# Layer 1's expert feed-forward, worked in smaller first groups, two experts at a time, and dealt out by amount of work

## The chip, the cores and the metric

The kernel runs on one core of one Trainium2 chip. The metric is device microseconds (us) for one execution. Three runs of the kernel before took 4180.68, 4183.84 and 4184.01 us; the median is 4183.84 us.

## The reference, cut to what matters

A graph of 6250 nodes (256 features each) and 100000 edges, sorted by destination node, goes through two layers. Each layer is a graph step and then a mixture of experts, and each adds to the node features `x`:

```python
x = x + L0_gnn(layernorm(x), ...)                # weighted graph convolution and a small MLP
x = x + L0_ffn(layernorm(x), ...)                # 8 experts, top 2
x = x + L1_gnn(edge_index, layernorm(x), ...)    # the table and sums below
x = x + L1_ffn(layernorm(x), ...)                # the feed-forward below

# L1_gnn: a table of 8 relations, gathered by edge and summed by destination
hx = einsum('ni,rio->rno', x, weight);  msg = hx[edge_type, src]
agg = segment_sum(msg, dst);  out = agg * 0.5**0.5 + h_bias + (x @ loop_weight) * 0.5**0.5

# L1_ffn: 6 experts of three 256x256 products each, all computed for every node
rh = relu(f @ router_w1 + b);  logits = softmax(rh @ router_w2 + b);  top 2, softmax of the two
h1 = relu(f @ w1[e] + b1[e]);  h2 = relu(h1 @ w2[e] + b2[e]);  y = h2 @ w3[e] + b3[e]
out = sum over the two chosen experts of weight * y
```

Here `f` is `layernorm(x)` after the graph step. A node's feed-forward can begin only when all of its edges have been summed.

## The kernel before, in words

Nodes lie in 49 tiles of 128. The kernel's stages follow each other: layer 0's messages and sums, its experts, the relation table `hx` (line 1425, matmuls from 2459.9 to 2907.8 us), and then the last stage, which the change touches and which runs from about 2913 us to the end.

In that last stage two things are interleaved. The function `aggregate` (line 906) makes 830 turns. A turn gathers 128 rows of the table with one indirect DMA, issued by POOL (line 920, tile `g1`, 10 buffers); multiplies them on PE by a 0/1 selection matrix `m1` with three bf16 matmuls (line 928, `pa1`); and adds the result to the accumulator of one node tile on DVE (line 932). The matrix `m1` is made on DVE once in 8 turns (line 912). Edges are sorted by node, so tile after tile is completed, one every 17 turns or so.

The other thing is layer 1's feed-forward over groups of node tiles. `FFN_GROUPS` lists the groups; before, they have 2 tiles, then eleven times 4, then 2 and 1. A group passes two generators. `prepare` (line 1466) adds the graph sums to the features, normalizes, transposes on PE (`pt_x3`), runs the router (`pqa`, `pl3`), the softmax and the top 2 (`route`, `shares`, on DVE and ACT; the result is the table of weights `C`), transposes `C` (`pc1`, line 1520) and adds the weighted bias (`pcb1`, line 1527). `experts1` (line 1533) then takes the six experts in turn: two dense products, in two halves each (`dense_steps`, line 470: `ph_e1` and `ph_e2` on PE, a relu on ACT, line 482, into `v1` and `v2`), and a third product for every tile (`mix`, line 1003: `py1` on PE, line 1007, and a multiply-add on DVE, line 1008). A `yield` ends a piece of it.

The PSUM pool `mm`, with 4 buffers, serves `pa1`, `ph`, `py1`, `pqa` and `pcb1` alike; whoever needs a buffer waits until ACT or DVE has read it out.

The function `layer1` (line 1555) decides the order. After each turn of `aggregate` it may start the next group's preparation, if that group's last tile is complete for certain (`TURNS * sum(waiting[0]) + SLACK <= turn`, that is turn 17 x tiles + 8) and fewer than `LIVE - 1` = 2 groups stand in the queue; it advances the running preparation by one step; and it deals out pieces of expert work from an account `due`, which grows each turn by `left / (T - turn + 40)`. Before, every piece counts as one, whatever its size: with 4 tiles all pieces hold two units of work, a unit being a pair of matmuls with 256 columns; with 2 tiles the dense pieces hold one unit. When the 830 turns are over, a loop empties the queue. The framework that builds the program may shift instructions within an engine's queue[...].

Of the kernel before, what the change touches and what calls it, by code (L numbers as in the profile page):

```python
# [8 lines left out]
F32 = mybir.dt.float32  # L9
# [5 lines left out]
AF = mybir.ActivationFunctionType  # L15
# [7 lines left out]
NT = 49  # L23
# [5 lines left out]
T = C_ + NT - 1  # L29
# [19 lines left out]
TABLE_GROUPS = [(0, 1)] + [(g, 4) for g in range(1, NT, 4)]  # L49

LIVE = 3
SIZES = [2] + [4] * 11 + [2, 1]
FFN_GROUPS = [(sum(SIZES[:i]), n) for i, n in enumerate(SIZES)]


@with_exitstack
def gnn_ffn_kernel(ctx: ExitStack, tc: tile.TileContext, a, out):
    nc = tc.nc
# [36 lines left out]
    last = N - (NT - 1) * 128  # L95
# [32 lines left out]
    col0, n = {}, 0  # L128
# [19 lines left out]
    def col(name, i=0):  # L148
        j = col0[name] + i
        return cols[:, j : j + 1]  # L150
# [66 lines left out]
    with tc.If(unsorted > 0):  # L217
        with tc.tile_pool(name="reorder", bufs=1) as rp:
# [22 lines left out]
            for c in range(EC):  # L241
                ins = nc.gpsimd.indirect_dma_start(
                    out=records,
# [69 lines left out]
    for q0 in range(0, QN, 4):  # L313
        n = min(4, QN - q0)
# [37 lines left out]
    turn = gap.tile([128, Q * 128], F32, name="turn")  # L352
# [35 lines left out]
    for q in range(Q):  # L388
        nc.gpsimd.indirect_dma_start(
            out=M[:, q].rearrange("p e r -> p (e r)"),  # L390
# [79 lines left out]
    def dense_steps(name, w, xT, ncols, func, bias, dest):  # L470

        for f in range(2):
            ps = psum_mm(f"ph_{name}_{f}")
            for k in range(2):
                nc.tensor.matmul(  # L475
                    ps[:, :ncols],
                    w[:, k, f * 128 : (f + 1) * 128],
                    xT[:, k, :ncols],
                    start=(k == 0),
                    stop=(k == 1),  # L480
                )
            nc.scalar.activation(dest[:, f, :ncols], ps[:, :ncols], func, bias=bias[f])  # L482
            yield
# [519 lines left out]
    def mix(s, t, i, e, C, hT, j, w):  # L1003

        ps = psum_mm(f"py{s}_{t}_{e}")
        for k in range(2):
            nc.tensor.matmul(ps[:, :D], hT[:, k, j : j + 128], w[:, k, :], start=(k == 0), stop=(k == 1))  # L1007
        nc.vector.scalar_tensor_tensor(  # L1008
            X[:, t, :], ps[:, :D], C[:, i, e : e + 1], X[:, t, :], op0=OP.mult, op1=OP.add
        )  # L1010
# [393 lines left out]
    tiles = []  # L1404
# [61 lines left out]
    def prepare(g, n, va, tag):  # L1466


        tiles = range(g, g + n)
        m = n * 128  # L1470
        mv = va.tile([128, n, 2], F32, name=f"mv3{tag}_{g}", tag="mv3", bufs=2)
        for i, t in enumerate(tiles):
            nc.vector.scalar_tensor_tensor(
                X[:, t, :], acc[:, t * D : (t + 1) * D], math.sqrt(0.5), X[:, t, :], op0=OP.mult, op1=OP.add
            )
            st = work.tile([128, 6], F32, name=f"st3{tag}_{t}", tag="st", bufs=3)
            nc.vector.bn_stats(st, X[:, t, :])
            nc.vector.bn_aggr(mv[:, i, :], st)
            yield
        rstd = va.tile([128, n], F32, name=f"rstd3{tag}_{g}", tag="rstd3", bufs=2)  # L1480
        inverse_root(f"ln3{tag}_{g}", va, mv[:, :, 1], rstd, n)
        yield
        xT = va.tile([128, 2, 512], F32, name=f"xT3{tag}_{g}", tag="xT3", bufs=LIVE)
        normed = []
        for i in range(n + 1):
            if i < n:
                t = g + i
                xn = work.tile([128, D], F32, name=f"xn3{tag}_{t}", tag="xn", bufs=3)
                nc.vector.tensor_scalar(
                    xn, X[:, t, :], mv[:, i, 0:1], rstd[:, i : i + 1], op0=OP.subtract, op1=OP.mult  # L1490
                )
                normed.append(xn)
            if i:
                transpose_to(f"x3{tag}_{g + i - 1}", xT[:, :, (i - 1) * 128 : i * 128], normed[i - 1])
            yield
        yield
        ps = psum_mm(f"pq{tag}{g}")
        for k in range(2):
            nc.tensor.matmul(ps[:, :m], qw1[:, k, :], xT[:, k, :m], start=(k == 0), stop=(k == 1))
        q = va.tile([128, 512], F32, name=f"q{tag}{g}", tag="q", bufs=1)  # L1500
        nc.scalar.activation(q[:, :m], ps[:, :m], AF.Relu, bias=col("L1_ffn_router_b1"))
        yield
        yield
        pl = psum_sm(f"pl3{tag}_{g}")
        for i in range(n):
            nc.tensor.matmul(
                pl[:, i * 8 : i * 8 + 6], q[:, i * 128 : (i + 1) * 128], qw2, start=True, stop=True
            )
        yield
        L = va.tile([128, n, 6], F32, name=f"L3{tag}_{g}", tag="L3", bufs=2)  # L1510
        nc.vector.tensor_add(
            L, pl[:, : n * 8].rearrange("p (n e) -> p n e", e=8)[:, :, :6], qb2.to_broadcast([128, n, 6])
        )
        C = shares(f"1{tag}{g}", va, n, 6, *(yield from route(f"1{tag}{g}", va, L, n, 6, True)))
        yield
        yield

        pc = psum_sm(f"pc1{tag}_{g}")
        for i in range(n):
            nc.tensor.transpose(pc[:6, i * 128 : (i + 1) * 128], C[:, i, :], ident)  # L1520
        cT = va.tile([8, 512], F32, name=f"cT1{tag}_{g}", tag="cT", bufs=1)
        nc.scalar.copy(cT[:6, :m], pc[:6, :m])
        yield
        yield
        for i, t in enumerate(tiles):
            ps = psum_mm(f"pcb1{tag}_{t}")
            nc.tensor.matmul(ps[:, :D], cT[:6, i * 128 : (i + 1) * 128], vb3, start=True, stop=True)
            nc.vector.tensor_add(X[:, t, :], X[:, t, :], ps[:, :D])
            if i % 2:
                yield  # L1530
        return xT, C

    def experts1(g, n, va, tag, xT, C):

        tiles = range(g, g + n)
        m = n * 128
        for e in range(6):
            h1 = va.tile([128, 2, 512], F32, name=f"v1{tag}_{g}_{e}", tag="actT", bufs=1)
            h2 = va.tile([128, 2, 512], F32, name=f"v2{tag}_{g}_{e}", tag="hid", bufs=1)
            b1 = [col("L1_ffn_expert_b1", 2 * e + f) for f in range(2)]  # L1540
            b2 = [col("L1_ffn_expert_b2", 2 * e + f) for f in range(2)]
            yield from dense_steps(f"e1{tag}_{g}_{e}", vw1[:, e], xT, m, AF.Relu, b1, h1)
            yield from dense_steps(f"e2{tag}_{g}_{e}", vw2[:, e], h1, m, AF.Relu, b2, h2)
            for i, t in enumerate(tiles):
                mix(f"1{tag}", t, i, e, C, h2, i * 128, vw3[:, e])
                if e == 5:
                    r = last if t == NT - 1 else 128
                    nc.sync.dma_start(out[t * 128 : t * 128 + r, :], X[:r, t, :])
                if i % 2 or i == n - 1:
                    yield  # L1550

    def pieces(n):
        return 6 * (4 + (n + 1) // 2)

    def layer1(tag, early):


        with tc.tile_pool(name=f"gather{tag}", bufs=1) as gp, tc.tile_pool(name=f"act{tag}", bufs=1) as va:
            waiting = list(FFN_GROUPS)
            prep, queue = None, []  # L1560
            left = sum(pieces(n) for _, n in waiting[:-2])

            def prepare_some():

                nonlocal prep
                if prep is None:
                    return False
                g, n, steps = prep
                try:
                    next(steps)  # L1570
                except StopIteration as end:
                    queue.append(experts1(g, n, va, tag, *end.value))
                    prep = None
                return True

            def experts_some():
                while queue:
                    if next(queue[0], queue) is not queue:
                        return True
                    queue.pop(0)  # L1580
                return False

            due = 0.0
            for turn in aggregate(gp, acc, hx, tag):
                if not early:
                    continue
                if prep is None and waiting and len(queue) < LIVE - 1 and TURNS * sum(waiting[0]) + SLACK <= turn:
                    g, n = waiting.pop(0)
                    prep = (g, n, prepare(g, n, va, tag))
                prepare_some()  # L1590
                due = min(due + left / (T - turn + 40), 1.5)
                while due >= 1 and experts_some():
                    due, left = due - 1, left - 1
            while prep or waiting or queue:
                if prep is None and waiting and len(queue) < LIVE:
                    g, n = waiting.pop(0)
                    prep = (g, n, prepare(g, n, va, tag))
                prepare_some()
                experts_some()
# [62 lines left out]
```

## Time and profile before

| what | value |
|---|---|
| median of three runs | 4183.84 us |
| the profiled execution's own time | 4184.38 us |
| its span, first to last instruction | 4182.6 us |
| PE / DVE / ACT / POOL busy over the span | 83% / 50% / 31% / 54% |
| last stage: first and last gather issued | 2920.3 and 4060.0 us |
| last stage: first and last matmul of the gathered sums | 2925.5 and 4073.8 us |
| first expert matmul (`ph_e1`) | 3008.0 us |
| last expert matmul (`py1`) | 4176.4 us |

Times inside the span are counted from its first instruction. The profile gives, per stretch of time, the busy time of each engine and the clock that TensorE was granted (1.00 is full speed). It also gives every instruction's start, so that the three `pa1` matmuls of a turn tell when PE reached that turn, and the gather's start tells when POOL did; the difference, in turns, is called the lead of the gathers below. It can't exceed the 10 buffers.

### The profile page before, as it was taken

Reading aid. Unit: us, or ns where it says so; the run is one execution under the profiler, and the core shown is the slowest. Engines: PE = TensorE matmul, PEld = TensorE weight load, DVE = VectorE, ACT = ScalarE, POOL = GpSimd, SP = SyncE. Lnnn points to the kernel's source line nnn. Section 1 sums busy time; section 2 is a strip of 40 time slices with the busy share of each in tenths; the row PEclk is TensorE's granted clock in tenths of the full one; section 3 lists DMA queues with packets and bytes.
Section 4 is the critical chain, followed back from the end, with each engine's and each line's share of the span. In section 5 each row is a group of like instructions: output and inputs, shape, how many; then the busy total and the mean of one; then the engine's idle time right before and its main releaser. Section 6 shows DMA issues by size and latency. Waiting matters only on the chain.

```text
span 4182.6 us, 53223 instructions
## 1 busy us (share of the span) xinstructions
PE 3478.2 (83%) x14645; PEld 2313.5 (55%) x14645; DVE 2083.1 (50%) x5720; ACT 1310.2 (31%) x2934; POOL 2261.2 (54%) x2440
## 2 busy tenths in 40 slices
PE   2887777777777568888969967998679999999999
PEld 1565656655656345555547733444356666666656
DVE  6686211111111146777853367664456666666652
ACT  3312333333333212333324434665012222222213
POOL 1001777777777524555550057333767777777750
PEclk8998999999999788999989988999689999999999
DMA  5514433333333434555643335445645555555540
GB/s 178 170 38 148 131 128 127 128 128 127 127 127 128 159 102 158 191 201 188 214 165 108 109 122 199 196 196 201 187 140 152 151 153 153 147 154 153 146 115 9
DMA packets 233067, 612.09 MB, mean 146 GB/s; under 512 B 41908, under 2 KB 126103, under 8 KB 212783
## 3 DMA queue, kind: packets, MB, share of 16 engines
q0 software_dynamic: 100624, 294.88, 22.7%
q1 hardware_dynamic: 112636, 290.21, 20.8%
q10 hardware_dynamic: 19488, 23.31, 1.6%
q8 instruction: 132, 2.16, 0.2%
q14 instruction: 187, 1.53, 0.1%
HBM read 371.49 MB, written 236.79 MB: 145 GB/s over the span
## 4 chain that ended last, share of the span: by engine, by line
PE 41%; DVE 12%; DMA 5%; issue 5%; POOL 2%; ACT 2%; DVEq 1%; ACTq 0%; SPq 0%; POOLq 0%
PE ph_e1a L475 6%; PE py1a L1007 6%; PE pa1a L928 6%; PE ph_e2a L475 5%; PE pa0e L901 4%; PE phx L1425 4%; DMA g0e<-msgs 3%; DVE acc L903 3%; PE pf L1344 2%; PE pf L1360 2%; DVE rest L1435 1%; DVE acc L932 1%; PE pt_fh L463 1%; DVE hx L1419 1%; PE pg2e L1094 1%
## 5 line engine op out<-in xcount | busy, mean ns | idle before, releaser
L860 POOL DMA_INDIRECT msgs<-msgn,at x782 | 787.4, 1007 | 550.3 <-DMA M<-edge_table,natq_i 313.6
L920 POOL DMA_INDIRECT g1a<-hx,idxT x830 | 828.6, 998 | 319.1 <-PE pa1a L928 142.5
L842 PE MATMUL pxn<-acc,sTn 128*128 x3128 | 792.2, 413 | 242.1 <-DVE sTn L823 215.3
L842 PEld LDWEIGHTS pxn<-acc,sTn 128*128 128x128 f32 x3128 | 613.9, 206 | 420.3 <-DVE sTn L823 282.2
L901 PE MATMUL pa0e<-g0e,m0e 128*128 128x256 f32 x1660 | 503.3, 436 | 157.5 <-DVE acc L903 71.8
L857 ACT ACTIVATE msgn<-pxn,ewT 128x256 f32<-128x256 f32 x782 | 370.1, 473 | 638.5 <-PE pxn L842 468.0
L932 DVE TENSOR_TENSOR acc<-acc,pa1a 128x256 f32 x830 | 346.7, 418 | 341.8 <-PE pa1a L928 309.8
L901 PEld LDWEIGHTS pa0e<-g0e,m0e 128*128 128x128 f32 x1660 | 293.0, 207 | 330.6 <-issue 128.5
L898 POOL TENSOR_SCALAR m0e<-minus,keye 128x128 f32<-128x128 f32 x414 | 259.5, 641 | 320.0 <-PE pa0e L901 275.7
L833 DVE COPY msgn<-srcT 128x32 f32<-128x32 f32 x98 | 17.5, 181 | 831.1 <-DMA msgs<-msgn,at 722.1
L928 PE MATMUL pa1a<-g1a,m1a 128*128 128x256 bf16 x2490 | 375.6, 283 | 51.6 <-DMA g1a<-hx,idxT 35.0
L928 PEld LDWEIGHTS <-m1a 128*128 128x128 bf16 x2490 | 244.0, 100 | 275.2 <-issue 192.3
L903 DVE TENSOR_TENSOR acc<-acc,pa0e 128x256 f32 x830 | 347.2, 418 | 92.7 <-PE pa0e L901 42.9
L1425 PE MATMUL phx<-wr,xT 128*128 128x512 f32 x784 | 368.5, 613 | 29.1 <-DVE rest L1435 21.6
L1007 PE MATMUL py1a<-w_L_ffn_expert_w,v2a 128*128 128x256 f32 x1176 | 286.6, 384 | 6.0 <-DVE acc L932 3.0
L475 PE MATMUL ph_e1a<-xT3a,w_L_ffn_expert_w 128*128 128x512 f32 (+2 forms) x672 | 287.9, 555 | 0.0
L475 PE MATMUL ph_e2a<-v1a,w_L_ffn_expert_w 128*128 128x512 f32 (+2 forms) x672 | 280.1, 542 | 2.1 <-DVE acc L932 1.3
L482 ACT ACTIVATE v1a<-ph_e1a,cols 128x512 f32<-128x512 f32 (+2 forms) x168 | 106.5, 634 | 538.8 <-PE ph_e1a L475 525.7
L1425 PEld LDWEIGHTS phx<-wr,xT 128*128 128x128 f32 x784 | 148.2, 197 | 188.5 <-issue 161.2
L1385 POOL DMA_INDIRECT y<-ys,ats x98 | 97.5, 995 | 277.5 <-issue 262.2
L1007 PEld LDWEIGHTS py1a<-w_L_ffn_expert_w,v2a 128*128 128x128 f32 x1176 | 208.8, 190 | 44.2 <-ACT v2a L482 10.3
L1008 DVE SCALAR_TENSOR_TENSOR X<-py1a,C1a,X 128x256 f32<-128x256 f32 x294 | 138.9, 480 | 112.3 <-PE py1a L1007 111.4
(646 smaller groups left out, 4373.2 us busy)
## 6 DMA issues: line engine op xcount, KB each, us to landing
g0e<-msgs SPq DMA_DIRECT2D x104, 1040.0 KB
hx<-hx SPq DMA_DIRECT2D x49, 1536.0 KB
rowsn<-lane_rows SPq DMA_DIRECT2D x98, 256.0 KB
fx<-xs SPq DMA_DIRECT2D x105, 128.0 KB
ys<-fy ACTq DMA_DIRECT2D x105, 128.0 KB
g1a<-hx,idxT POOLq DMA_INDIRECT x830, 3.1
msgs<-msgn,at POOLq DMA_INDIRECT x782, 2.4
msgs<-none ACTq DMA_DIRECT2D x10, 650.0 KB
```

What stands on the lines that cost most here:

```text
L475: nc.tensor.matmul(ps[:, :ncols], w[:, k, f * 128 : (f + 1) * 128], xT[:, k, :ncols], start=(k == 0), stop=(k == 1),)
L842: nc.tensor.matmul(come, sT[:, k, j, :], acc[:, bass.ds(blocks[j] * D + k * D, D)], start=(k == 0), stop=(k == 1),)
L857: nc.scalar.activation(msg[:, j, :D], come, AF.Copy, scale=ewT[:, t0 + j : t0 + j + 1])
L860: ins = nc.gpsimd.indirect_dma_start(out=msgs, out_offset=bass.IndirectOffsetOnAxis(ap=at[:, t0 + j : t0 + j + 1], axis=0), in_=msg[:, j, ...
L898: nc.gpsimd.tensor_scalar(m[:, j], minus, key[:, j : j + 1], None, op0=OP.is_equal)
L901: nc.tensor.matmul(ps[:, :D], m[:, j, :], g[:, j, :D], start=True, stop=True)
L903: nc.vector.tensor_add(here, here, ps[:, :D])
L920: nc.gpsimd.indirect_dma_start(out=g, out_offset=None, in_=table, in_offset=bass.IndirectOffsetOnAxis(ap=idxT[:, t0 + j : t0 + j + 1], axi ...
L928: nc.tensor.matmul(ps[:, :D], m[:, j, :], g[:, k * D : (k + 1) * D], start=(k == 0), stop=(k == 2))
L932: nc.vector.tensor_add(here, here, ps[:, :D])
L1007: nc.tensor.matmul(ps[:, :D], hT[:, k, j : j + 128], w[:, k, :], start=(k == 0), stop=(k == 1))
L1425: nc.tensor.matmul(ps, xT[:, k, :], wr[:, k, r : r + 2, :].rearrange("p r o -> p (r o)"), start=(k == 0), stop=(k == 1),)
```

## The change

Four edits. The groups begin smaller: 1, 2, 2, 3 tiles, then nine times 4, then 2, 2, 1. In groups of one or two tiles `experts1` takes two experts together: both first products, then both second products, then both mixes, side by side in the same `v1` and `v2` buffers; larger groups go through the same sequence as before. A piece now hands out its size in units of work, the account of `layer1` counts these units, may run up to 3.0, and deals while it is above zero. And `prepare` has one more `yield` between the weights `C` and their transpose, so that a preparation lasts one turn longer.

```diff
-SIZES = [2] + [4] * 11 + [2, 1]
+SIZES = [1, 2, 2, 3] + [4] * 9 + [2, 2, 1]
 FFN_GROUPS = [(sum(SIZES[:i]), n) for i, n in enumerate(SIZES)]
...
         C = shares(f"1{tag}{g}", va, n, 6, *(yield from route(f"1{tag}{g}", va, L, n, 6, True)))
         yield
         yield
+        yield
...
     def experts1(g, n, va, tag, xT, C):
         tiles = range(g, g + n)
         m = n * 128
-        for e in range(6):
-            h1 = va.tile([128, 2, 512], F32, name=f"v1{tag}_{g}_{e}", tag="actT", bufs=1)
-            h2 = va.tile([128, 2, 512], F32, name=f"v2{tag}_{g}_{e}", tag="hid", bufs=1)
...
-            yield from dense_steps(f"e1{tag}_{g}_{e}", vw1[:, e], xT, m, AF.Relu, b1, h1)
-            yield from dense_steps(f"e2{tag}_{g}_{e}", vw2[:, e], h1, m, AF.Relu, b2, h2)
-            for i, t in enumerate(tiles):
-                mix(f"1{tag}", t, i, e, C, h2, i * 128, vw3[:, e])
...
-    def pieces(n):
-        return 6 * (4 + (n + 1) // 2)
+        some = 2 if n <= 2 else 1
+        for e0 in range(0, 6, some):
+            h1 = va.tile([128, 2, 512], F32, name=f"v1{tag}_{g}_{e0}", tag="actT", bufs=1)
+            h2 = va.tile([128, 2, 512], F32, name=f"v2{tag}_{g}_{e0}", tag="hid", bufs=1)
+            parts = [(e0 + c, slice(256 * c, 256 * c + m)) for c in range(some)]
+            for e, cs in parts:
+                b1 = [col("L1_ffn_expert_b1", 2 * e + f) for f in range(2)]
+                for _ in dense_steps(f"e1{tag}_{g}_{e}", vw1[:, e], xT, m, AF.Relu, b1, h1[:, :, cs]):
+                    yield n / 2
+            for e, cs in parts:
+                b2 = [col("L1_ffn_expert_b2", 2 * e + f) for f in range(2)]
+                for _ in dense_steps(f"e2{tag}_{g}_{e}", vw2[:, e], h1[:, :, cs], m, AF.Relu, b2, h2[:, :, cs]):
+                    yield n / 2
+            for e, cs in parts:
+                for i, t in enumerate(tiles):
+                    mix(f"1{tag}", t, i, e, C, h2, cs.start + i * 128, vw3[:, e])
...
+                    if i % 2 or i == n - 1:
+                        yield 1 + i % 2
...
-            left = sum(pieces(n) for _, n in waiting[:-2])
+            left = sum(18 * n for _, n in waiting[:-2])
...
-                due = min(due + left / (T - turn + 40), 1.5)
-                while due >= 1 and experts_some():
-                    due, left = due - 1, left - 1
+                due = min(due + left / (T - turn + 40), 3.0)
+                while due > 0:
+                    piece = experts_some()
+                    if not piece:
+                        break
+                    due, left = due - piece, left - piece
```

`experts_some` returns the size of the piece that it dealt, or 0.

More of the change, by code (lines that the diff above doesn't have):

```diff
@@ L1536, in experts1 @@
         m = n * 128
-        for e in range(6):
-            h1 = va.tile([128, 2, 512], F32, name=f"v1{tag}_{g}_{e}", tag="actT", bufs=1)
-            h2 = va.tile([128, 2, 512], F32, name=f"v2{tag}_{g}_{e}", tag="hid", bufs=1)
-            b1 = [col("L1_ffn_expert_b1", 2 * e + f) for f in range(2)]
-            b2 = [col("L1_ffn_expert_b2", 2 * e + f) for f in range(2)]
-            yield from dense_steps(f"e1{tag}_{g}_{e}", vw1[:, e], xT, m, AF.Relu, b1, h1)
-            yield from dense_steps(f"e2{tag}_{g}_{e}", vw2[:, e], h1, m, AF.Relu, b2, h2)
-            for i, t in enumerate(tiles):
-                mix(f"1{tag}", t, i, e, C, h2, i * 128, vw3[:, e])
[L1546 to L1550, printed above, removed]
-    def pieces(n):
-        return 6 * (4 + (n + 1) // 2)
+        some = 2 if n <= 2 else 1
[14 more added lines that the diff above has]
+                    mix(f"1{tag}", t, i, e, C, h2, cs.start + i * 128, vw3[:, e])
+                    if e == 5:
+                        r = last if t == NT - 1 else 128
+                        nc.sync.dma_start(out[t * 128 : t * 128 + r, :], X[:r, t, :])
+                    if i % 2 or i == n - 1:
+                        yield 1 + i % 2
     def layer1(tag, early):
@@ L1577, in experts_some @@
                 while queue:
-                    if next(queue[0], queue) is not queue:
-                        return True
+                    piece = next(queue[0], 0)
+                    if piece:
+                        return piece
                     queue.pop(0)
-                return False
+                return 0
             due = 0.0
```

## The prediction

> **What bounds the kernel now.** I read the page's slices first; everything up to 2913 us is the same in both programs. In the last stage I asked for busy times by stretch, then for the waits of PE and POOL, then for single instructions. Busy times by stretch (PE, weight loads, DVE, ACT, POOL, each with its count; granted clock; DMA share; GB/s):
>
> ```profile
> 2920.00:2960.00 40.00, 21.86 (x84) 8.90 (x84) 16.82 (x33) 0.00 (x0) 30.58 (x31) 0.50 0.84 265
> 2960.00:3000.00 40.00, 24.09 (x102) 11.52 (x103) 20.66 (x61) 2.71 (x5) 30.62 (x31) 0.56 0.55 153
> ...
> 3080.00:3120.00 40.00, 27.90 (x113) 15.16 (x112) 21.19 (x76) 4.89 (x11) 23.36 (x25) 0.74 0.44 126
> 3200.00:3400.00 200.00, 199.22 (x933) 124.05 (x934) 126.53 (x338) 42.29 (x69) 148.14 (x147) 1.00 0.54 153
> ...
> 4040.00:4050.00 10.00, 9.88 (x22) 5.11 (x23) 2.75 (x7) 0.75 (x2) 2.66 (x3) 0.50 0.28 79
> ```
>
> First PE is idle or at half clock while POOL gathers; at 3080 both lose; from 3200 PE is full at full clock; at 4040 PE is slow. POOL's own cadence and one slow gather (start, us, what):
>
> ```profile
> 3031.44 0.95 POOL L920 DMA_INDIRECT g1a<-hx,idxT  x1 [0.30 <-PE pa1a L928]
> 3032.69 1.97 POOL L920 DMA_INDIRECT g1a<-hx,idxT  x1 [0.30 <-PE pa1a L928]
> ```
>
> Alone a gather costs 0.95 + 0.30 = 1.25 us. With the slow ones it is 1.31 us: gather 266 starts at 3281.8 us, the first at 2920.3, and 14 us of that are waits on PE (part 1), so (361.5 - 14) / 266. From 3294 to 3846 us PE takes 1.36 us a turn (406 turns in 552.6 us): PE binds there, but POOL is only 4% behind. POOL's longest wait from 3078 to 3240 us (us in total, times, longest), and PE's waits from 3009 to 3080 us and then from 3130 to 4065 us:
>
> ```profile
> POOL g1a L920 <- PE pa1a L928: 27.1, 48, 3.5
> ```
>
> ```profile
> PE pa1a L928 <- ACT v2a L482: 7.1, 12, 0.6
> PE pa1a L928 <- ACT v1a L482: 2.2, 5, 0.6
> ...
> PE pc1a L1520 <- DVE C1a L1000: 5.8, 3, 4.0
> ```
>
> Of POOL's 27.1 us, 48 x 0.30 are its own issue time; 12.7 are lost to PE. With the two-tile group PE waits for PSUM buffers that ACT still reads; later for the weights `C` of the groups at tiles 38 and 42, when expert work has run out before their transpose. And the end, two experts of the last one-tile group (start, us, what):
>
> ```profile
> 4161.71 1.13 PE L1007 MATMUL py1a<-w_L_ffn_expert_w,v2a 128*128 128x256 f32 x4 [0.23 <-ACT v2a L482]
> 4165.19 1.13 PE L1007 MATMUL py1a<-w_L_ffn_expert_w,v2a 128*128 128x256 f32 x4 [0.23 <-ACT v2a L482]
> ```
>
> An expert takes 3.48 us there, part of it waiting for its own relus.
>
> **The skill.** The Trainium skill, *TensorE: Matmul & The Clock Gate*, § HAM oscillation, says that idle gaps over about 3.4 us put PE back to half clock; the trace agrees: 4.3 us before `pc1` at 4038.9, then 0.50. *GPSIMD Engine Reference*, § 1. Specifications: GpSimd shares SBUF interfaces with VectorE operations that have two SBUF inputs; the 1.97 us gather stands beside line 912 on DVE (1.23 us from 3032.6). *Perfetto Trace Analysis*, § Matmuls: matmul groups should rotate through PSUM banks so that evacuation overlaps; the 9.3 us above are where four buffers shared by all do not do it.
>
> **The change, part by part.** I split PE's time from the first to the last matmul, 2925.5 to 4176.8 us, at turns 266 and 829, and count PE's work in each part from the order in which the two built programs put instructions on PE: 0.107 us per bf16 matmul of 256 columns (six `pa1` take 0.65 us in the full stretch), 0.43 and 0.216 us per f32 record of 512 and 256 columns (8 of them start within 3.43 and 1.73 us), an f32 matmul being two records. This work is 1107 us in both programs: nothing is removed from PE, only its waiting can change.
>
> | part | before | work in it, before | work, after |
> |---|---|---|---|
> | turns 0 to 265 | 368.1 | 262.4 | 260.5 |
> | 266 to 828 | 780.0 | 751.1 | 755.5 |
> | tail | 103.2 | 93.6 | 91.1 |
>
> *Part 1.* Expert work now begins at turn 41 instead of 60, and by turn 140 stands at 85 units (of 882) against 46; but groups wait for their tiles: it runs out in turns 56 to 78, 144 to 165 and 213 to 236 (before: 115 to 133), and by turn 260 both stand at 174 units. So the early start fills idle PE time, and pays only through POOL's waits. Before, POOL waited on PE beyond its 0.30 us for 9.4 us in gathers 115 to 149, 3.9 in 150 to 234, about 1 to 265: 14 us. After, I count the lead of the gathers, which blocks POOL above ten: a preparation on an idle PE costs the first group (2 tiles) 6 turns (lead 3 to 9), the second (4 tiles, 3088.2 to 3115.0 us for 12 turns, against 15.7 of POOL's) 11 us or 8.6 turns. Starting from lead 3: tile 0 and tiles 1 to 2 stay within ten. Turns 78 to 111: work 1.305 us a turn, and 11 PSUM waits on ACT in the order, 6.4 us (0.73 us from matmul to free buffer), make 1.49 against 1.31, so +6.1 us, lead 9 to 13.7: 4.8 us blocked. Then 1.2 a turn and a dry stretch bring it back to 3. Tiles 5 to 7: about 7 turns, 1 us blocked. Tiles 8 to 11: 8.6 turns, lead 11.6 to 12.6, 3 us. Sum 9 against 14: -5; and the lead at turn 266 is 8.5 instead of 10: -2. **-7 us.**
>
> *Part 2.* Work +4.4 (preparations come later, more units before the tail). PSUM and ACT waits in the order, 5.5 us before, 8.3 after: +2.8. The added `yield` puts a preparation's end one turn later, and the gap in the expert work between groups is 5, 5, 5, 6, 6, 6, 7, 8 turns, before 3, 3, 3, 3, 3, 4, 4, 5, 5, 7. What counts is how many turns are dry before `pc1`: before, the group at 38 had 3 and lost 4.9 us (turns 740 to 780: 56.3 against 51.4), that at 42 had 5 and lost 10.7; those with 0 or 1 lost about 1. After: 1, 1, 1, 2, 2, 2, 4 and 6: the last two cost what those two cost, and 1.5 us are added for the rest. **+8.7 us**, 4.4 of them moved.
>
> *Tail.* Work -2.5. A group of 2 takes 5.61 us an expert (4133.06 to 4138.66) against 24 x 0.216 = 5.18; a group of 1 takes 3.48 against some 2.93 (16 records of 128 columns at 0.1225, its weight loads binding, and one mix of 0.97). The difference is waiting for relus, and two experts together cover it: 6 x 0.43 + 6 x 0.55 = -5.9. The second two-tile group is paired too and costs nothing extra: a 0.19 us weight load hides under 0.216. **-8.4 us.**
>
> *At nothing:* two more groups' small vector operations, some 70 of 0.18 us, 12 us of DVE, hidden under PE while DVE is 63% busy (126.5 of 200); on PE's path they would cost those 12. 56 more relus of at most 0.47 us on an ACT that is 21% busy. Output transfers, gathers and POOL's instructions keep number and order. Behind a later `pc1` stand the next turns' `pa1`, and POOL behind their buffers; that is counted in part 2.
>
> Sum -7 + 8.7 - 8.4 = -6.7: 4184.4 becomes 4177.7 in the profiled execution, 0.5 above the median of the runs; I say **4177**.
>
> **Rivals.** *Forecast*, 0.45, own range 4172 to 4185. *POOL runs free*, 0.25: the dry stretches let PE catch up, no gather waits, and the slow gathers become rare, as in gathers 20 to 59 (1.27 us each instead of 1.31): 250 x 0.04 = 10 us less, and half of the 9 us of blocking: 4163. For it: the lead of 3 whenever PE is dry. Against: gathers 60 to 114 took 1.33 at less PE load. *No gain in front*, 0.17: four preparations at half clock cost as much as the one removed; the +7 returns: 4184. *Slower*, 0.13: PE waits for `C` in every four-tile group. The price is that of group 38, 4.9 us, in the three groups with 2 dry turns (+14), 8 and 13 in the last two (+5): 4196. It decides when `pc1` waits exceed 25 us from turn 266 to 829. For it: 0 and 3 dry turns differ by 4 us; against: the added turn gives DVE 1.3 us more. *The change doesn't do what it says:* excluded for the start of the work, since the order shows it; pieces of four tiles are dealt as before, two units each.
>
> **How the numbers follow.** 0.2% is 8.4 us, about what a measurement of this kernel can tell from no change: below 4175.5 or above 4192.2. Faster: 0.13 of the forecast's 0.45, and all of the second: 0.38. Slower: the 0.13 and 0.01 more: 0.14. The rest 0.48. Range 4163 to 4193.
>
> **What would show it.** First expert matmul near 2981 us (turn 41), not 3008; gather 266 some 5 us earlier than 3281.8; clock near 0.5 in three dry stretches before turn 236; `pc1` waiting for `C` at the groups at tiles 36 and 40, little at 12 to 32; no PE wait for `v1` or `v2` in the tail, its small groups at 5.2 us an expert for 2 tiles. I am wrong if POOL's waits to turn 266 are not below 14 us, or if `pc1` waits in many groups.

## The result, and the profile after

The changed kernel takes **4211.72 us** (median of 6 runs, 4208.12 to 4214.56), the kernel before 4183.51 us beside it (6 runs, 4180.68 to 4190.83). The ratio is 1.0065 with a 95% interval of 1.0052 to 1.0077: slower by 0.65%, outside the predicted range and of the other sign. The profiled execution of the changed kernel has a span of 4207.1 us, against 4182.6.

I split both traces as the prediction did. *Front* is turns 0 to 265, *middle* 266 to 828, both by the start of a turn's first `pa1` matmul; *tail* runs from turn 829 to the last matmul. "POOL's waits" is what the gathers up to number 270 waited beyond their own 0.30 us.

| us | front | middle | tail | POOL's waits |
|---|---|---|---|---|
| before | 368.1 | 780.0 | 103.2 | 13.8 |
| after | 399.4 | 787.4 | 92.6 | 51.9 |
| difference | +31.3 | +7.4 | -10.6 | +38.1 |
| predicted difference | -7 | +8.7 | -8.4 | -5 |

The sum of the stages moves by +28.1. The middle and the tail came out near the forecast; the front grew by 31 us where a fall of 7 was forecast, and POOL's waits grew by 38 where a fall of 5 was forecast. The same views as before the change, now of the kernel after. Busy times by stretch (PE, weight loads, DVE, ACT, POOL, each with its count; granted clock; DMA share; GB/s):

```profile
2920.00:2960.00 40.00, 22.20 (x90) 9.38 (x90) 17.91 (x42) 0.00 (x0) 30.86 (x31) 0.54 0.81 258
2960.00:3000.00 40.00, 29.78 (x171) 23.14 (x172) 18.70 (x64) 9.31 (x25) 28.05 (x30) 0.73 0.53 145
...
3080.00:3120.00 40.00, 37.28 (x192) 29.51 (x193) 19.92 (x62) 9.35 (x22) 21.92 (x24) 0.91 0.42 117
...
3160.00:3200.00 40.00, 34.21 (x149) 21.17 (x148) 19.39 (x59) 6.12 (x12) 23.15 (x24) 0.80 0.39 109
...
3240.00:3280.00 40.00, 27.96 (x123) 16.93 (x122) 25.58 (x89) 3.55 (x9) 27.74 (x30) 0.73 0.56 156
...
3320.00:3520.00 200.00, 198.37 (x915) 123.10 (x914) 123.88 (x331) 41.25 (x68) 146.42 (x146) 0.99 0.53 149
```

POOL's column is the one to read. A stretch of 40 us holds 30 or 31 gathers when nothing stops POOL; here it holds 24 at 3080, where the kernel before has 25, and 24 again at 3160, where the kernel before has 32:

```profile
3160.00:3200.00 40.00, 39.68 (x189) 24.77 (x187) 28.26 (x95) 9.66 (x18) 29.11 (x32) 1.00 0.53 148
```

From 3120 to 3280 the kernel before was at full clock, with a PE busy for 39.7 to 40 of 40 us; the kernel after still falls back to 0.80 and 0.73 at 3160 and 3240. From 3320 both look alike.

What PE waited for in the front, before (2920 to 3294 us) and then after (2920 to 3321 us); us in total, times, longest:

```profile
PE pt_x3a L463 <- DVE xn3a L1489: 8.9, 2, 4.6
PE pc1a L1520 <- DVE C1a L1000: 8.3, 2, 4.5
...
PE pa1a L928 <- DVE acc L932: 6.8, 14, 1.2
```

```profile
PE pa1a L928 <- DVE acc L932: 18.1, 22, 2.0
PE pc1a L1521 <- DVE C1a L1000: 16.1, 5, 4.1
PE pt_x3a L463 <- DVE xn3a L1489: 15.7, 5, 4.6
```

There are five long waits of each kind where there were two: of the four preparations that began in the front before, two found PE with enough queued ahead of them; of the five now, none did. A preparation makes PE wait twice for a chain of small operations on DVE: for the normalized features `xn3`, and for the weights `C`. With the smaller waits inside a preparation (`pqa`, `pcb1`) this is 36.7 us against 19.3: +17.4. PE's idle time in the front (the front less PE's busy time in it) rose by 17.1, from 58.8 to 76.0 us. That the two numbers are so near is in part chance, since other waits moved too and nearly cancel: `pa1` waits 11.3 us more for an accumulator's addition, 7.6 less for relus on ACT, 3.7 less for gathers. The first of these belongs to the preparations as well. The additions stand on DVE among a preparation's first operations and the making of `m1`, as here, five microseconds before the `pt_x3` shown below (start, us, what):

```profile
3012.74 1.22 DVE L912 TENSOR_TENSOR m1a<-lanes_h,dlocT 128x1024 bf16<-128x1024 bf16 x1
3013.89 0.42 DVE L1477 BATCH_NORM_STATS2 st3a<-X 128x6 f32<-128x256 f32 x1
3014.22 0.40 DVE L932 TENSOR_TENSOR acc<-acc,pa1a 128x256 f32 x1
3014.68 0.49 PE L928 MATMUL pa1a<-g1a,m1a 128*128 128x256 bf16 x3 [1.97 <-DVE acc L932]
```

The rest of the 31.3 us is PE's own time, 323.4 against 309.3 us for work that is about equal at full clock: the mean granted clock of the front fell from 0.86 to 0.83, and 323.4 x 0.83 = 268 against 309.3 x 0.86 = 266. (This mean counts idle time too; the clock over PE's busy time alone gives 277 against 275.)

One of these preparations, for the group at tiles 1 and 2, while no expert work is left; PE, then POOL (start, us, what):

```profile
3019.95 1.11 PE L463 MATMUL pt_x3a<-ident,xn3a 128*128 128x128 f32 x4 [4.09 <-DVE xn3a L1489]
3021.53 2.08 PE L1499 MATMUL pqa<-xT3a,w_L_ffn_router_w 128*128 128x256 f32 x4 [0.46 <-ACT xT3a L465]
3023.40 1.49 PE L928 MATMUL pa1a<-g1a,m1a 128*128 128x256 bf16 x6
```

```profile
3020.09 0.94 POOL L920 DMA_INDIRECT g1a<-hx,idxT  x1 [0.30 <-issue]
3024.52 0.94 POOL L920 DMA_INDIRECT g1a<-hx,idxT  x1 [3.49 <-PE pa1a L928]
```

PE's queue is in order. `pt_x3` waits 4.09 us for DVE, then `pqa` runs at half clock (2.08 us for 4 records); the `pa1` of the next turns stand behind both, though their rows have been fetched. POOL, ten gathers ahead, stops for 3.49 us. The Trainium skill says so too: in *PSUM — Partial Sum Buffer*, § Engine vs sequencer instructions, weight loads on TensorE may overlap matmuls in flight, but matmuls start in program order. Fifteen microseconds later the new group meets a full account, PE first and then POOL:

```profile
3038.54 5.09 PE L475 MATMUL ph_e1a<-xT3a,w_L_ffn_expert_w 128*128 128x256 f32 x12
```

```profile
3044.23 0.94 POOL L920 DMA_INDIRECT g1a<-hx,idxT  x1 [4.26 <-PE pa1a L928]
```

Three pieces come in one turn, at half clock, and POOL waits 4.26 us more. Sorted by what stood on PE, some 22 of the 51.9 us are at such bursts, some 12 at the matmuls of a preparation itself, the rest in short waits. The sorting is rough: one wait of 5.4 us, at 3079 us, holds matmuls of both kinds.

The tail, last experts of the one-tile group (start, us, what):

```profile
4188.81 1.89 PE L1007 MATMUL py1a<-w_L_ffn_expert_w,v2a 128*128 128x256 f32 x8
4190.54 1.95 PE L475 MATMUL ph_e1a<-xT3a,w_L_ffn_expert_w 128*128 128x128 f32 x16
4192.32 1.95 PE L475 MATMUL ph_e2a<-v1a,w_L_ffn_expert_w 128*128 128x128 f32 x16
4194.11 1.89 PE L1007 MATMUL py1a<-w_L_ffn_expert_w,v2a 128*128 128x256 f32 x8
```

Two experts take 5.30 us (4188.81 to 4194.11), 2.65 each instead of 3.48, with no wait for a relu.

### The profile page after: what moved, and what is told of

It reads as the page before. It is cut to its first block, busy times and chain, and to the rows that moved or that the text cites. A ratio compares the mean times of both kernels' runs of the same rounds, so it can differ in the third digit from the quotient of the medians.

```text
span 4207.1 us, 53752 instructions
## 1 busy us (share of the span) xinstructions
PE 3488.9 (83%) x14845; PEld 2353.0 (56%) x14845; DVE 2085.2 (50%) x5794; ACT 1324.4 (31%) x2990; POOL 2254.4 (54%) x2440
## 4 chain that ended last, share of the span: by engine, by line
PE 41%; DVE 12%; DMA 5%; issue 5%; POOL 2%; ACT 1%; DVEq 1%; SPq 0%; ACTq 0%; POOLq 0%
PE ph_e1a L475 6%; PE ph_e2a L475 5%; PE pa1a L928 5%; PE py1a L1007 5%; PE pa0e L901 4%; PE phx L1425 4%; DMA g0e<-msgs 3%; DVE acc L903 2%; PE pf L1344 2%; PE pf L1360 2%; DVE rest L1435 1%; DVE acc L932 1%; DMA g1a<-hx,idxT 1%; PE pt_fh L463 1%; PE pcb1a L1528 1%
## 5 line engine op out<-in xcount | busy, mean ns | idle before, releaser
L928 PE MATMUL pa1a<-g1a,m1a 128*128 128x256 bf16 x2490 | 376.4, 282 | 53.3 <-DMA g1a<-hx,idxT 31.3
L475 PE MATMUL ph_e1a<-xT3a,w_L_ffn_expert_w 128*128 128x512 f32 (+3 forms) x768 | 297.9, 522 | 1.3 <-DVE acc L932 0.8
L475 PE MATMUL ph_e2a<-v1a,w_L_ffn_expert_w 128*128 128x512 f32 (+3 forms) x768 | 281.7, 497 | 1.1 <-ACT v2a L482 0.7
L482 ACT ACTIVATE v1a<-ph_e1a,cols 128x512 f32<-128x512 f32 (+3 forms) x192 | 112.7, 587 | 529.2 <-PE ph_e1a L475 528.4
```

Source lines behind the costliest of these rows:

```text
L475: nc.tensor.matmul(ps[:, :ncols], w[:, k, f * 128 : (f + 1) * 128], xT[:, k, :ncols], start=(k == 0), stop=(k == 1),)
L928: nc.tensor.matmul(ps[:, :D], m[:, j, :], g[:, k * D : (k + 1) * D], start=(k == 0), stop=(k == 2))
```

## The experiments

Three theories for the front. **D**: each preparation that falls on a PE without expert work costs 8 to 12 us (in-order waits for DVE, half clock, catching up). **B**: the account, allowed to run to 3.0, deals three units at once on a slow PE. **S**: small groups are slow by themselves. The table gives the stage times of each run's trace; ratios are to the kernel before, with 95% intervals.

| run | median us | ratio | front | middle | tail | POOL's waits |
|---|---|---|---|---|---|---|
| cap 1.5 | 4191.48 | 1.0020 [1.0013, 1.0027] | 392.9 | 772.2 | 94.3 | 41.3 |
| old sizes | 4191.86 | 1.0021 [1.0014, 1.0028] | 375.1 | 789.5 | 96.0 | 22.2 |
| new sizes alone, in the kernel before | 4231.60 | 1.0117 [1.0097, 1.0137] | 368.5 | 839.7 | 93.8 | 17.7 |
| without the yield | 4221.79 | 1.0097 [1.0077, 1.0116] | 397.5 | 798.6 | 92.6 | 48.2 |
| filler matmuls | 4211.65 | 1.0064 [1.0047, 1.0081] | 400.4 | 788.0 | 92.6 | 52.7 |
| no pairs | 4219.64 | 1.0087 [1.0069, 1.0106] | 395.3 | 787.5 | 101.7 | 46.2 |
| pairs alone, in the kernel before | 4183.36 | 0.9996 [0.9989, 1.0004] | 372.6 | 783.7 | 96.0 | 20.4 |
| old sizes, cap 1.5 | 4183.00 | 0.9995 [0.9986, 1.0004] | 373.7 | 779.4 | 96.2 | 20.0 |
| even dealing, new sizes | 4187.35 | 1.0017 [1.0007, 1.0026] | 388.3 | 775.8 | 94.1 | 39.6 |
| even dealing, old sizes | 4156.24 | 0.9947 [0.9930, 0.9963] | 360.2 | 766.3 | 98.2 | 8.0 |
| later steps | 4200.72 | 1.0050 [1.0033, 1.0067] | 386.7 | 790.3 | 92.6 | 37.8 |
| even, new sizes, later steps | 4180.69 | 0.9994 [0.9987, 1.0001] | 377.6 | 781.7 | 94.1 | 30.9 |
| even, old sizes, later steps | 4161.34 | 0.9953 [0.9936, 0.9971] | 362.0 | 773.4 | 98.2 | 8.6 |
| even dealing alone, in the kernel before | 4170.34 | 0.9967 [0.9953, 0.9981] | 367.0 | 768.2 | 105.5 | 11.5 |

A stage time comes from one profiled execution each. A stage with the same work and no edit still differs by up to about 4 us (the middle with pairs alone: 3.7), so smaller differences are not read. A stage also gets shorter when work leaves it: where the expert work done before turn 266 differs by more than 3 us, the text says so.

### The account's limit

```diff
-                due = min(due + left / (T - turn + 40), 3.0)
+                due = min(due + left / (T - turn + 40), 1.5)
```

> The changed kernel, with the account of expert work capped at 1.5 units instead of 3.0. In the changed kernel POOL waits 51.8 us on PE up to gather 270 (13.8 in the kernel before). Theory D (each preparation that falls on a PE without expert work, at half clock, costs 8 to 12 us, and there are four of them now): the dry preparations stay, waits stay at 45 us or more, time 4206 to 4212. Theory B (the account, full after a dry stretch, deals three units in one go at half clock while all ten gather buffers are full; four such places hold 18 us of the waits): waits fall to 35 to 42 us, time 4195 to 4202. Theory S (groups of 1 to 3 tiles are themselves slow to work through beside the gathers): no change, 4211.

Against the kernel after, the front gains 6.5 us and the middle 15.2. In the built order the expert work then runs out later: before `pc1` it is dry for 0, 0, 0, 0, 1, 1, 2 and 3 turns in the last eight four-tile groups, where the kernel after has 1, 1, 1, 2, 2, 2, 4 and 6. So the limit costs some 20 us in all, but in the front only 6.5 of the 31.3 us: B is a part, not the cause.

### The sizes, taken back, and alone

```diff
-SIZES = [1, 2, 2, 3] + [4] * 9 + [2, 2, 1]
+SIZES = [2] + [4] * 11 + [2, 1]
```

> The changed kernel with the group sizes of the kernel before (2, eleven times 4, 2, 1); pairs of experts, counting by units, cap and the added turn stay. Theory D: two dry preparations as before, of 2 and 4 tiles, so POOL's waits to gather 270 come to 14 to 22 us, turn 266 is reached 368 to 376 us after the first matmul (before 368.1, changed 399.4), time 4180 to 4190 with the shorter tail. Theory B: three full bursts at most, waits 20 to 25 us, time 4185 to 4195. Theory S: the sizes are the whole cause, waits 14 us, time 4178 to 4186.

The front gains 24.3 us of the 31.3 and POOL's waits fall from 51.9 to 22.2; the middle stays as slow as with the change. The reverse, the new sizes as the only edit of the kernel before:

> The kernel before with the new group sizes alone: no pairs, every piece counts one, cap 1.5, no added turn. In this one the slow count spreads the small groups so that expert work never runs out before turn 570; it runs out for 8, 10 and 13 turns before the last four-tile groups, and 146 instead of 174 units are done at turn 260. Theory D: POOL's waits to gather 270 fall to 5 to 12 us, turn 266 at 345 to 360 us; but the late dry gaps cost 5, 10 and 12 us, and 28 units (24 us) are still to do, so time 4185 to 4205. Theory S: small groups beside the gathers cost by themselves, waits over 30 us, turn 266 at 385 us or later although less work is done, time 4215 or more. Theory B: no bursts, as D.

Here the front is *not* slower (368.5), though it has the same five preparations. Its account counts pieces, and pieces of small groups hold less work: by turn 260 it has dealt 28 units fewer. PE's busy time in the front is 296.0 us instead of 309.3, so that its waits (24 us in the preparations) find room, and POOL waits 17.7 us in it. The bill comes later: the middle takes 59.7 us more. Some 36 of these are expert work that moved there from the front and the tail, counted by the records in the traces at the prediction's prices. The rest fits the work running out before the last groups: POOL waits 102.7 us in the middle, against 45.7 before, and PE waits for `C` again (waits from 3320 to 4100 us):

```profile
PE pc1a L1520 <- DVE C1a L1000: 14.3, 5, 5.6
```

So the new sizes cost the front their 24 us only at the rate of dealing that comes with the account of units. Here the front is nearly as long as POOL alone makes it: 266 gathers at 1.31 us and the 17.7 us of waits are 366 us.

### The yield

```diff
         yield
         yield
-        yield
```

> The changed kernel without the added turn in a preparation. Theory D: the front keeps its four dry preparations, waits 45 us or more to gather 270; gaps between groups are 5 to 7 instead of 5 to 8 turns, worth 0 to 4 us; time 4207 to 4212. A rival, that the added turn is what hurts because it lengthens every dry stretch: time 4200 or less.

Without the yield the kernel is 10 us slower, the middle by 11: PE's waits for `C` there rise from 1.8 us (1 wait) to 5.8 (4), all its waits inside preparations from 7.1 to 13.7; the rest is PE's busy time, 4.9 us more at a lower clock (0.981 for 0.989). The extra turn for DVE is worth more than the turn of expert work that it delays. I had counted it as a cost.

### Filler matmuls in dry turns

```diff
+                dry = not queue
...
+                if dry and turn >= 20:
+                    pf = p_tr.tile([128, 2, 128], F32, tag="tr", name=f"fill{tag}_{turn}")
+                    nc.tensor.matmul(
+                        pf.rearrange("p a b -> p (a b)"), ident, vw1[:, 0, 0, :], start=True, stop=True
+                    )
```

The filler's result is used by nobody.

> The changed kernel plus one unread 256-column f32 matmul (0.43 us at full clock) in every turn from 20 on in which no group is ready for expert work. It only adds work to PE; if time falls, it can only be by the clock. Theory D with the half clock as its core: the clock in the dry stretches before turn 240 rises from 0.5 to 0.7 towards 1.0, POOL's waits to gather 270 fall from 51.8 to 25 to 35 us, turn 266 is reached 375 to 385 us after the first matmul instead of 399.4, time 4185 to 4198. If the lost time is PE waiting in order for DVE and ACT (the chain of a preparation), and not the clock: waits 48 us or more, time 4208 to 4220.

The granted clock of the dry stretches rose (0.59 to 0.67 in 2940 to 2980 us, 0.64 to 0.87 in 3145 to 3183) and the time did not move. *TensorE: Matmul & The Clock Gate*, § HAM oscillation, names idle gaps over about 3.4 us as what puts PE back to half clock, and for thin matmuls advises a loop order that keeps PE busy. The clock rose as this would have it, but the gap's length differs here: in the kernel after, full clock ends at 3080.8 us after two waits of 1.82 and 0.46 us. And what fills the gaps takes its own time on the same in-order queue, 0.43 us each at full clock. The half clock alone is thus not shown to be the cause; this filler doesn't remove it either.

### Pairs

```diff
-        some = 2 if n <= 2 else 1
+        some = 1
```

> The changed kernel with one expert at a time in all groups. Tail from turn 829 to the last matmul: 92.6 us with pairs, so 98 to 101 without (5.9 more by my count of the relu waits). Front: if pairs make the small groups slow in turns 78 to 111 (1.80 us a turn), turn 266 comes earlier than 399.4 us; if they help there, as counted, it comes 3 to 10 us later. Time 4217 to 4228 by theory D, 4200 to 4212 if pairs hurt the front.

The tail loses 9.1 us without pairs, and the whole some 9 (0.22% by the ratios). Pairs as the only edit of the kernel before (the new `experts1` without sizes in its yields):

> The kernel before with two experts at a time in groups of one or two tiles, nothing else. Front and middle as before (368 and 780 us), tail 103.2 to 97: time 4176 to 4179, by all theories; if pairs hurt beside the gathers, the first group, worked in turns 60 to 115, shows it: turn 266 later than 372 us, time 4183 or more.

The tail gains 7.2 us, yet the median equals that of before. Front and middle read 4.5 and 3.7 us more; that is at the scatter of single traces, so where the 7 us went stays open.

### Old sizes and the lower limit together

The two edits at the top in one kernel; what remains of the change is the pairs, the yield and the account in units.

> The changed kernel with the sizes of the kernel before and the account capped at 1.5. Theory D and B together: two dry preparations (front 370 to 376 us), smaller bursts (middle 770 to 776, as with cap 1.5 and new sizes, where it was 772.3 against 787.4), tail 95: sum 1235 to 1247 against 1251.3 before, time 4168 to 4180, faster than both kernels. If the middle's gain with cap 1.5 came from the sizes and not from the cap, middle 785 or more, time 4184 to 4190.

This equals the kernel before: each edit alone gained 20 us, both 28.7. They partly heal the same thing.

### Even dealing

If D holds, the work should never run out. The rate of dealing is also held to the units that are ready, divided by the turns to the next group's first expert work; the limit is 1.5.

```diff
+                    ready.append(18 * n)
...
-                due = min(due + left / (T - turn + 40), 3.0)
+                coming = prep or (waiting[0] if waiting else None)
+                rate = left / (T - turn + 40)
+                if coming:
+                    start = TURNS * (coming[0] + coming[1]) + SLACK + 15 + 5 * coming[1] // 2
+                    rate = min(rate, sum(ready) / max(1, start - turn))
+                due = min(due + rate, 1.5)
...
+                    ready.append(-piece)
```

> The changed kernel with the cap of the account at 1.5, and with the dealing rate held to (units ready) / (turns to the next group's expert work), so that expert work no longer runs out before a preparation; same groups, same early start, same pairs. Theory D (a preparation that falls on a PE without expert work costs 8 to 12 us, because PE waits in order for DVE's chain and then catches up): POOL's waits to gather 270 fall from 51.9 to 20 us or less, turns 0 to 265 take 365 to 375 us, turns 266 to 828 765 to 775, the tail 93; 4165 to 4180 us. Theory S (small groups, or the bursts that an account of units makes, are slow by themselves): turns 0 to 265 take 385 us or more, and the time stays at 4185 or above.

The miss that taught most. After the first group no stretch is dry any more (at most 3 turns without expert work between groups), and the front still takes 388.3 us; D as I had put it falls. The half clock doesn't carry it either: the mean granted clock of this front is 0.88, above the 0.86 of the kernel before. But S as a whole does not follow: all of POOL's waits over 0.5 us lie between turns 65 and 113, with two preparations. PE in the second one:

```profile
3080.97 0.49 PE L928 MATMUL pa1a<-g1a,m1a 128*128 128x256 bf16 x3 [0.17 <-DVE acc L932]
3084.19 1.09 PE L463 MATMUL pt_x3a<-ident,xn3a 128*128 128x128 f32 x4 [2.74 <-DVE xn3a L1489]
3085.74 2.08 PE L1499 MATMUL pqa<-xT3a,w_L_ffn_router_w 128*128 128x256 f32 x4 [0.46 <-ACT xT3a L465]
3087.61 3.32 PE L1007 MATMUL py1a<-w_L_ffn_expert_w,v2a 128*128 128x256 f32 x8
3090.77 0.82 PE L928 MATMUL pa1a<-g1a,m1a 128*128 128x256 bf16 x6
```

There is expert work, and it stands *behind* `pt_x3` in the queue. From 3080.97 to 3090.77 no turn starts. A preparation costs its in-order waits whether the stretch is dry or not. The same dealing with the old sizes:

> The same dealing with the old groups (2, eleven times 4, 2, 1). Theory D: turns 0 to 265 take 365 to 370 us, 266 to 828 about 770, the tail 96; 4165 to 4178 us, the fastest so far. Theory S expects it at least 15 us below the kernel with the same dealing and the new groups.

4156.24 us, the fastest of the study: 0.53% below the kernel before. (The fronts with even dealing hold 3.4 us less expert work than those of the kernels before and after, 16 records of `py1`.) It too has `pt_x3` waits of up to 4.9 us in its front, but few preparations, far apart, and POOL waits 8.0 us. In the middle, PE's waits for `C` are gone (waits from 3290 to 4050 us):

```profile
PE pt_x3a L463 <- DVE xn3a L1489: 1.0, 3, 0.7
...
PE pc1a L1521 <- DVE C1a L1000: 0.4, 1, 0.4
```

### Later steps in the preparation

Four more turns between the normalization and `pt_x3`, three more before `pc1`, for the groups that begin before tile 12; the rest is the kernel after.

```diff
+        if g < 12:
+            yield
+            yield
+            yield
+            yield
         xT = va.tile([128, 2, 512], F32, name=f"xT3{tag}_{g}", tag="xT3", bufs=LIVE)
...
+        if g < 12:
+            yield
+            yield
+            yield
         pc = psum_sm(f"pc1{tag}_{g}")
```

> The changed kernel with four more turns between a preparation's normalization and its transposes on PE, and three more before the transpose of C, for the groups that begin before tile 12. If in a dry preparation the loss is PE's waiting in order for DVE's chain (pt_x3 for xn3, pc1 for C), POOL's waits to gather 270 fall from 51.9 to 30 us or less, and turns 0 to 265 take 385 us or less instead of 399.4; 4195 to 4202 us. If the loss is the burst of expert work after it, or the half clock, nothing changes beyond 4 us: 4208 to 4216.

PE's waits from 2928 to 3315 us in this run:

```profile
PE pc1a L1530 <- DVE C1a L1000: 9.3, 4, 3.5
...
PE pt_x3a L463 <- DVE xn3a L1494: 3.2, 3, 1.9
```

The two kinds together fall by 19.3 us, from 31.8 to 12.5, the front by 12.7 and POOL's waits by 14.1, which misses both marks that I had set (386.7 for 385, 37.8 for 30). And the 12.7 us are not all won. PE's busy time in the front fell by 7.0 of them, because the later preparations push expert work behind turn 266 (16 records of `py1` and 8 of `ph_e2` with 512 columns, 6.9 us at the prediction's prices). PE's idle time fell by 5.7 only: where the in-order waits went, `pa1` waits longer for relus (9.2 us for 1.7) and for gathers (43.2 for 31.3). The ratio goes from 1.0065 to 1.0050, with intervals that overlap. So this run shows some 6 of the front's 31 us to hang on the in-order waits; it doesn't show them to be the main part.

### Both, with a control, and the even dealing alone

The same later steps on top of the even dealing (with `start` put 7 turns later for these groups), with the new sizes and, before tile 10, with the old; and the even dealing as the only edit of the kernel before, counted in pieces.

> The evenly dealt kernel with the new groups and the later steps again, hoped to be on a chip on which the kernel before takes 4180 us and not 4513. Waiting for DVE's chain as the cause of the front's rest: waits for xn3 and C to turn 266 of 8 us or less, POOL's waits to gather 270 of 22 or less, turns 0 to 265 at 372 us or less; 4170 to 4178 us. The small groups' own expert work: 380 us or more in turns 0 to 265, 4180 or above.

> The control with the old groups again: turns 0 to 265 between 350 and 358 us, 4146 to 4155 us; if PE's waits are hidden behind POOL's lead there: 4153 to 4159.

> The kernel before with the even dealing alone, again. If the even dealing alone makes the gain: turns 0 to 265 take 358 to 363 us, 266 to 828 764 to 769, the tail 103; 4158 to 4166 us. If it needs the account of units or the added turn: 4172 or above.

The three were run once before on a chip that is slower for every kernel, the kernel before included (4513 us); the ratios there were 1.0012, 0.9969 and 0.9990, in the same order of kernels, and its stage times are not used.

With the new sizes the front falls from 388.3 to 377.6 us, between my two marks: 5.6 us of waits for `xn3` and `C` are left, but POOL still waits 30.9. About 5 us of the fall are again expert work that moved behind turn 266, and the middle grows by 5.9; the ratio, 0.9994 for 1.0017, shows a gain all the same. What is left over the control (377.6 - 362.0 = 15.6 us, with nearly equal work in the two fronts) shows in the small groups' own work. One turn of a two-tile group (start, us, what):

```profile
3075.32 0.47 ACT L482 ACTIVATE v2a<-ph_e2a,cols 128x256 f32<-128x256 f32 x1 [1.50 <-PE ph_e2a L475]
3075.84 0.49 PE L928 MATMUL pa1a<-g1a,m1a 128*128 128x256 bf16 x3 [0.62 <-ACT v2a L482]
...
3077.76 0.49 PE L928 MATMUL pa1a<-g1a,m1a 128*128 128x256 bf16 x3 [0.56 <-DMA g1a<-hx,idxT]
```

`pa1` starts 0.05 us after the relu of the `ph` ahead of it has ended, so it waits for ACT. The last line names a gather as the releaser, but POOL is ten gathers ahead there and the next relu ends at 3077.70 us: the name is wrong, the time fits the relu. A turn takes 1.92 us. Counting every `pa1` that starts within 0.13 us of a relu's end after an idle PE: 44 in this front, 22.0 us, against 21 and 11.3 in the control. As PE's idle time that is 10.7 of the 15.6 us; the waits inside preparations are 8.7 against 4.0 us, 4.7 more. By this count S holds for this part; no run takes the relu waits away, so it is argued and not shown. In the kernel after, with its bursts, there are only 4 such waits (2.3 us): there the smaller groups' cost stands at preparations and in the clock, in the even version at relus.

The control shows that later steps bring the old sizes nothing (0.9953 against 0.9947, the intervals overlap), which fits PE's waits being covered where POOL waits 8 us only. The even dealing alone makes 0.9967, at 4170.34 us a few above what I had named for it: its middle has the whole gain (768.2, in the mark), its front little of it (367.0 for 358 to 363). The best version is 0.20% below it, some 8 us, with intervals that just overlap; the tail of 105.5 against 98.2, which pairs shorten, would make most of that.

## Why the prediction was wrong

**What failed: part 1, the count of POOL's blocking.** It put 9 us of blocking where 51.9 were measured.

- It took two prices from the trace, 6 turns of lead for a preparation of two tiles and 8.6 for four, let nearly each preparation begin from a lead of about 3, and had the lead fall back between them. Measured, the lead was 3 before the first preparation (turn 28), but 7, 10, 7 and 4 before the next four (turns 63, 99, 150 and 220), so that little room was left. And from there to turns 41, 78, 112, 165 and 237, behind its last matmuls, each cost more turns than such a preparation was priced at: 10.2, 11.6, 11.1, 13.6 and 14.2 us beyond 1.31 us a turn, which is 8 to 11 turns. One tile costs 10 us and four cost 14.
- For turns 78 to 111 it took 1.49 us a turn from work and relu waits. They took 1.80: the stretch holds another preparation, that of tiles 3 and 4 (from turn 99 on), whose waits the sum left out, and bursts at half clock.
- It held that early expert work only fills idle PE time. It does, but the early groups brought five preparations with long waits to the front (7.3 us each) where the trace of before shows two. Two things that come with them had no term of their own: `pa1` waiting for additions on DVE (18.1 us for 6.8), and bursts of three units at half clock behind a preparation.

The rival named *No gain in front* came nearest, with preparations that eat the gain. Its size was off, for it ended at no gain; and it put the cost on the half clock, which the runs don't show to be the cause: with even dealing and the new sizes the front still took 20 us more than before, at a higher clock. *POOL runs free* was the opposite of what came. *Slower* had the right sign for another reason: `pc1` waits from turn 266 to 829 are 1.8 us, not the 25 at which it was to decide.

**Part 2** has a sum that is about right (+7.4 against +8.7) out of terms that were not. The waits for `C` did not grow with 4 and 6 dry turns, which fits the yield giving DVE its turn; PE's idle time even fell by 0.9 us. All of the difference is PE's busy time, 776.5 against 768.2: 4.4 is work, as counted, and the other 3.9 stay open, at the scatter of single traces (the mean clock of the middle is 0.989 in both). That the sum came out is luck. The yield counted as a cost; taken out, the time rose by 10 us.

**The tail** was right in mechanism and size: no wait for `v2`, 5.18 us an expert with 2 tiles (two in 10.36, 4164.52 to 4174.88) as forecast, and 2.65 instead of the forecast 2.93 with one tile.

**The signs.** The first expert matmul came at 2979.8 us (forecast near 2981), so the work did start early. Gather 266 came 29.4 us later, not 5 earlier. The clock near 0.5 came in part: the 33 to 41 us around each of the three dry stretches after turn 41 have means of 0.64 to 0.71, with pieces at half clock in each, as here:

```profile
3034.00:3043.00 9.00, 7.66 (x20) 5.30 (x21) 2.06 (x11) 1.31 (x3) 4.11 (x5) 0.50 0.43 126
```

`pc1` waited at the group at tile 40 (1.76 us), but not at that at tile 36. One reading of the trace of before was off: PE's idle time before `pc1` at 4038.9 is 3.99 us, not 4.3. Of the things that I said would prove me wrong, POOL's waits above 14 us did.

## What to carry to other kernels

When a change cuts work into more, smaller groups, count what each group costs *once*: here a chain of small operations on one engine that another waits for in the middle of an in-order queue, paid mostly per group and not per tile. Price it where the buffers are already full, since the same five preparations cost the front nothing in the version whose PE had less work in it. And when a stage gets faster, look whether work has left it. Holding the rate of dealing to what is ready, with the old sizes, made the only versions here that are faster than the kernel before.

## What the runs showed that I had not expected

- With filler matmuls in every dry turn the clock around the dry stretches rose to 0.67 to 0.87, not to 1.00, and no time was won.
- A turn with one `ph` of 256 columns takes 1.92 us, though its matmuls take 1.2 at full clock, because `pa1` waits for the relu of the `ph` just ahead of it, 0.56 to 0.62 us each.
- Two edits that each won 20 us (smaller limit, old sizes) won 28.7 together, and the best version, which keeps the pairs, the yield and the units but not the new sizes, runs in 0.9947 of the time before.
